# Paired row halves, kept x pieces, a held convolution and a joined start in a two-layer image kernel

## The chip, the cores and the metric

The kernel runs on one core of a Trainium2 chip. The metric is the device time of one execution in microseconds; the median of three executions stands for a kernel. A profile is one further execution, with its own time.

## The reference

Two layers, each `x + conv(groupnorm(x))` on `x` of 4 images x 192 channels x 128 x 128, all in fp32. Cut to what matters:

```python
# layer 0
x1 = _c1x1(x, conv1_w)                       # 192 -> 48 channels
x_0, x_05, x_1 = x1[:, :16], x1[:, 16:32], x1[:, 32:48]
Fre = _frft2d(x_05, 0.5)                     # fractional Fourier transform
mag, pha = abs(Fre), angle(Fre)
mag_out = _c1x1(_c3x3(mag * mask1) * mask1 + _c1x1(mag * mask2) * mask2)
ifrft = abs(_frft2d(complex(mag_out * cos(pha_out), mag_out * sin(pha_out)), -0.5))
fre = rfft2(x_1)                             # ordinary Fourier transform
x_1o = irfft2(...)                           # 1x1 convolutions of its magnitude and phase
x = x + _c1x1(concat([x_0o, ifrft, x_1o]), conv2_w)   # 48 -> 192 channels

# layer 1: a selective scan over the 16384 pixels of each image
seq = layernorm(groupnorm(x)); xs, z = split(seq @ in_proj)       # 384 + 384
u = silu(causal_conv4(xs)); dt, Bm, Cm = split(u @ x_proj)
dt = softplus(dt @ dt_proj + b)
h = h * exp(dt * A) + (dt * u) * Bm;  y = sum(h * Cm)             # 16 states
x = x + ((y + u * D) * silu(z)) @ out_proj
```

## The kernel before

**Layer 0** (`layer0`) works image by image, in generators that a loop at its end advances in turns. A scheduler then orders the recorded instructions on each engine; every engine, and every queue of an engine that issues transfers, works in the order that comes out. Nearly all loads are issued by SP, the stores of `d1` by ACT and the stores of `xmid` by POOL.

- `analysis(b)` has two passes over the image's 16 pieces of 8 rows (`PIECE` = 1024 pixels, two tiles of 96 channels side by side: 768 KB each). The first takes the group statistics (`bn`, line 192), the second loads every piece again and makes the 48 channels with line 278, whose matmuls use one column half of the array for each half piece. The result goes to `d1` in DRAM.
- `branches(b)` is the Fourier part. It has 26 steps (`yield`s): 8 in the forward transforms (lines 214 and 224, `spectrum`; the polar form of each half is lines 76 to 96, with the magnitude's sum on POOL, line 78), 4 in the convolutions (line 348 is the 3x3 one), 2 in the second branch's 1x1 convolutions, 8 in the inverse fractional transform (lines 407 to 421) and 4 in the inverse ordinary one (lines 437 to 448). It ends with the write of `dimg` to DRAM (line 453).
- `synthesis(b)` loads the x pieces a third time. For each piece it loads `cat`, which has 49 rows: 16 of `d1`, 32 of `dimg` and a row of ones (lines 464 to 466). Four matmuls with 49 rows (line 471) make 192 channels of 1024 pixels, DVE adds them to x (line 475), takes statistics for layer 1 (line 192), and POOL stores the piece to `xmid` (line 477).

All x pieces come from one pool of six tiles, `l0x`. While `branches(b)` runs, the loop advances `analysis(b+1)` once in every step and once more in odd steps, and `synthesis(b-1)` in even steps; what is left of both is flushed after it. For the last image there is no analysis ahead, so only the synthesis of image 2 runs beside its branches. `synthesis` of the last image runs alone.

**Layer 1** (`layer1`) has its order written out by hand. The 128 chunks of 512 pixels pass through `front` (a generator of 34 steps: normalisation, projections, convolution, `dt`), then 24 positions of scans. In the main loop `front(n+2)` starts at position 14 (`FRONT`) of chunk n, does ten steps there and the remaining 24 in the next chunk. To start, `front(0)` runs through, then the inputs of the first scans are prepared, and then ten steps of `front(1)` are done before the loop begins. `NGR` is 24.

Of the kernel before, what the change touches and what calls it, by code (L numbers as in the profile page):

```python
# [10 lines left out]
F32 = mybir.dt.float32  # L11
# [8 lines left out]
C = 192  # L20
CH = 96
GROUP = 6
NC = 16
# [9 lines left out]
PIECE = ROWS * S  # L33
NPIECE = S // ROWS
# [87 lines left out]
def layer0(tc, x, xmid, st2, w):  # L122

    nc = tc.nc
    B = x.shape[0]
    with ExitStack() as ctx:
# [10 lines left out]
        qp = pool("l0q", 1)  # L137
# [22 lines left out]
        nc.sync.dma_start(out=w2x[0:NC, :], in_=folded[0:NC, :])  # L160
        nc.sync.dma_start(out=w2x[3 * NC :, :], in_=folded[NC:, :])
        half_pi = cp.tile([128, 1], F32, name="half_pi")
        nc.vector.memset(half_pi, math.pi / 2)

# [4 lines left out]
        dmag = []  # L169
        zrow = cp.tile([1, S], F32, name="zrow")  # L170
        nc.vector.memset(zrow, 0.0)
        orow = cp.tile([1, PIECE], F32, name="orow")
        nc.vector.memset(orow, 1.0)
# [73 lines left out]
        def analysis(b, got):  # L247


            st = sp.tile([CH, 2, NPIECE * (PIECE // 512), 6], F32, name="st")  # L250
            for p in range(NPIECE):
                bn(st, p, load(b, p))
                yield
            gst = sp.tile([CH, 2, 2], F32, name="gst")
            bn_done(st, gst)

            w1r = sp.tile([CH, 2, 128], F32, name="w1r")
            for t in range(2):  # L260
                nc.vector.tensor_scalar(w1r[:, t, :], w1T[:, t, :], gst[:, t, 1:2], None, ALU.mult)
            ps = psA.tile([128, 512], F32, name="ps")
            for t in range(2):
                nc.tensor.matmul(
                    ps[:, 0:1], w1r[:, t, :], gst[:, t, 0:1], start=t == 0, stop=t == 1
                )
            b1 = sp.tile([128, 1], F32, name="b1")
            nc.vector.tensor_scalar(b1, ps[:, 0:1], -1.0, None, ALU.mult)
            d1 = got["d1"] = dram.tile([3 * NC, S * S], F32, name="d1")
            for p in range(NPIECE):  # L270
                xt = load(b, p)
                if p % 2 == 0:
                    x1 = sp.tile([128, 2, 512], F32, name="x1")
                ps = psA.tile([128, 512], F32, name="ps")
                for t in range(2):
                    for q in range(2):
                        half = slice(64 * q, 64 * (q + 1))
                        nc.tensor.matmul(
                            ps[half], w1r[:, t, half], xt[:, t, q * 512 : (q + 1) * 512],
                            start=t == 0, stop=t == 1,  # L280
                        )
# [171 lines left out]
            nc.sync.dma_start(out=dimg.rearrange("c h w -> h c w"), in_=img)  # L453
            got.update(dimg=dimg)

        def synthesis(b, got):

            d1, dimg = got["d1"], got["dimg"].rearrange("c h w -> c (h w)")
            st = sp.tile([CH, 2, NPIECE * (PIECE // 512), 6], F32, name="st2")
            for p in range(NPIECE):  # L460
                xt = load(b, p)
                cat = qp.tile([3 * NC + 1, PIECE], F32, name="cat", bufs=2)
                at = slice(p * PIECE, (p + 1) * PIECE)
                nc.sync.dma_start(out=cat[0:NC, :], in_=d1[0:NC, at])
                nc.sync.dma_start(out=cat[NC : 3 * NC, :], in_=dimg[:, at])
                nc.sync.dma_start(out=cat[3 * NC :, :], in_=orow)
                for q in range(PIECE // 512):
                    at = slice(q * 512, (q + 1) * 512)
                    pr = psB.tile([128, 2, 512], F32, name="pr")
                    for t in range(2):  # L470
                        nc.tensor.matmul(  # L471
                            pr[0:CH, t, :], w2x[:, t * CH : (t + 1) * CH], cat[:, at],
                            start=True, stop=True,
                        )
                    nc.vector.tensor_add(xt[:, :, at], xt[:, :, at], pr[0:CH])  # L475
                bn(st, p, xt)
                nc.gpsimd.dma_start(  # L477
                    out=split(xmid[b][:, p * PIECE : (p + 1) * PIECE]), in_=xt
                )
                yield  # L480
            bn_done(st, st2[:, b])
# [3 lines left out]
        got = [{} for _ in range(B)]  # L485
        for _ in analysis(0, got[0]):
            pass
        behind = iter(())
        for b in range(B):
            ahead = analysis(b + 1, got[b + 1]) if b + 1 < B else iter(())  # L490
            for i, _ in enumerate(branches(b, got[b])):
# [5 lines left out]
            behind = synthesis(b, got[b])  # L497
        for _ in behind:
            pass

# [3 lines left out]
def layer1(tc, xmid, out, st2, w, n_tok=S * S):  # L504

    nc = tc.nc
    B = len(xmid)
    NCHUNK = n_tok // T
    G = 2
    LAG, FRONT, BCL = 3, 14, 5  # L510
# [4 lines left out]
    MID, LATE = "mid", "late"  # L515
# [3 lines left out]
    with ExitStack() as ctx:  # L519
        def pool(name, bufs, **kw):  # L520
            return ctx.enter_context(tc.tile_pool(name=name, bufs=bufs, **kw))

        cp = pool("l1c", 1)
        dram = pool("l1d", 3, space=DRAM)
        xp = pool("l1x", 3)
# [66 lines left out]
        NG = NS // G  # L592
        NGR = NJ * NG
        got = [{} for _ in range(total)]
# [355 lines left out]
        fronts = []  # L950

        def start_front(n):
            if n < total:
                fronts.append(front(n))

        def step(works, parts):

            for f in list(works):
                got_on = next(f, f)
                if got_on is f:  # L960
                    works.remove(f)
                elif got_on is not None:
                    parts[got_on].append(f)

        def go_on(parts, part):

            for f in parts[part]:
                got_on = next(f, None)
                if got_on is not None:
                    parts[got_on].append(f)  # L970

        with tc.manual_schedule():
# [12 lines left out]
            decay_there(2)  # L985


            start_front(1)
            for _ in range(NGR - FRONT):
                parts = {MID: [], LATE: []}  # L990
                step(fronts, parts)
                go_on(parts, MID)
                go_on(parts, LATE)
            tails = []
            for pos, (n, k) in enumerate(order):
                j, sg = divmod(k, NG)
# [4 lines left out]
                parts = {MID: [], LATE: []}  # L1001
# [188 lines left out]
```

## Time and profile before

| | us |
|---|---|
| median of three executions | 11470.67 (11470.17 to 11471.05) |
| the profiled execution | 11449.58 |
| its span | 11447.4 |
| analysis of image 0 alone ends (load of `img` issued) | 126.4 |
| writes of `dimg`, images 0, 1, 2, 3 | 395.9, 699.2, 1029.8, 1302.6 |
| first constant of layer 1 | 1436.5 |
| first scan of layer 1 | 1515.3 |

Busy shares of the whole span are PE 92%, DVE 92%, POOL 86%, ACT 81%: those are layer 1's. In layer 0 the shares change from stretch to stretch, and must be read there. In lines of the timeline the columns are start, length, engine, line, operation, what is written and read, the shape and the count; in brackets is the idle time just before and what ended it. An engine name ending in q is that engine's issue queue. An fp32 matmul shows as two passes.

### The profile page before, as it was taken

To read this page: it belongs to the slowest core of one execution; us is meant where nothing else is said; L and a number is where in the kernel's file an instruction comes from. 1 tells how busy PE (TensorE), PEld (TensorE's weight loads), DVE (VectorE), ACT (ScalarE), POOL (GpSimd) and SP (SyncE) were. 2 spreads that over 40 slices of the span, in tenths; PEclk is the share of its full clock that TensorE was granted. 3 is DMA by queue.
4 is the path that set the end of the run, shared out by engine and by line. 5 is a ranking of instruction groups with operands and counts; after the bars stand their busy time and mean duration, and the time that the engine had idled before them with its cause. 6 is when DMAs were issued, how large, how long until landed. Compare 5 with 4: busy or idle time off the path is not lost.

```text
span 11447.4 us, 163662 instructions
## 1 busy us (share of the span) xinstructions
PE 10543.1 (92%) x54154; PEld 7050.4 (62%) x54154; DVE 10489.8 (92%) x11072; ACT 9324.7 (81%) x17508; POOL 9806.5 (86%) x4470
## 2 busy tenths in 40 slices
PE   4777889999999999999999999999999999999998
PEld 2444456666666666666666666666666666666666
DVE  5665679999999999999999999999999999999999
ACT  2322179988988998998998998898899999889887
POOL 0000069999999999999999999999999999999999
PEclk8888789999999999999999999999999999999998
DMA  8787734334334434434433433443443443344343
GB/s 209 206 223 203 196 106 128 112 119 128 118 113 128 127 106 130 128 107 124 128 112 119 128 120 111 128 127 105 129 128 109 123 128 114 117 128 121 111 128 99
DMA packets 1339431, 1494.73 MB, mean 131 GB/s; under 512 B 903473, under 2 KB 954358, under 8 KB 1338070
## 3 DMA queue, kind: packets, MB, share of 16 engines
q1 hardware_dynamic: 1318102, 1421.34, 42.7%
q0 software_dynamic: 13312, 50.34, 1.3%
q10 hardware_dynamic: 7168, 12.59, 0.3%
q8 instruction: 429, 7.03, 0.2%
q14 instruction: 420, 3.44, 0.1%
HBM read 1325.19 MB, written 155.32 MB: 129 GB/s over the span
## 4 chain that ended last, share of the span: by engine, by line
ACT 29%; DVE 29%; PE 26%; issue 10%; POOL 3%; DMA 2%; DVEq 0%; ACTq 0%; POOLq 0%; SPq 0%
DVE h L872 21%; ACT da L802 9%; ACT dbT L846 6%; DVE op L822 6%; PE py L898 5%; PE ps L666 4%; PE ps L936 4%; PE ps L685 4%; ACT L802 3%; PE op L858 2%; POOL db L830 2%; ACT op L802 2%; PE pr L471 2%; ACT L693 1%; PE ps L655 1%
## 5 line engine op out<-in xcount | busy, mean ns | idle before, releaser
L885 POOL TENSOR_TENSOR hc<-h,bc 128x1024 f32<-128x1024 f32 x3072 | 7196.8, 2373 | 230.7 <-PE ps L922 145.6
L872 DVE TENSOR_TENSOR_SCAN h<-da,carry,op 128x512 f32<-128x512 f32 x4216 | 5202.2, 1262 | 18.7 <-ACT da L802 7.1
L898 PEld LDWEIGHTS py<-ident,hc 128*128 128x128 f32 x24576 | 3001.5, 148 | 849.3 <-issue 685.1
L898 PE MATMUL py<-ident,hc 128*128 128x128 f32 x24576 | 3404.1, 285 | 29.9 <-ACT yt L907 17.5
L802 ACT ACTIVATE da<-dt,c_A_log 128x512 f32<-128x512 f32 x4352 | 2994.6, 724 | 184.3 <-DVE h L872 163.6
L872 DVE TENSOR_TENSOR_SCAN h<-op,carry,db 128x512 f32<-128x512 f32 x1736 | 2202.3, 1269 | 119.2 <-POOL db L830 115.2
L830 POOL TENSOR_TENSOR db<-dtu,bc 128x1024 f32<-128x1024 f32 x896 | 2136.3, 2384 | 5.6 <-DMA bc<-dbc 5.6
L822 DVE TENSOR_TENSOR op<-dp,bc 128x512 f32<-128x512 f32 x2816 | 1889.9, 671 | 32.2 <-ACT dp L785 32.2
L802 ACT ACTIVATE op<-dt,c_A_log 128x512 f32<-128x512 f32 x1792 | 1223.2, 683 | 679.7 <-DVE h L872 674.4
L846 ACT ACTIVATE dbT<-ps,bT 128x128 f32<-128x128 f32 x6144 | 1660.3, 381 | 0.0
L666 PE MATMUL ps<-s,c_wiT 96*128 96x512 f32 x3072 | 1520.9, 619 | 2.6 <-DVE s L660 2.6
L685 PE MATMUL ps<-xs,dcw 128*128 128x512 f32 x3072 | 1424.3, 592 | 1.5 <-ACT u L693 1.3
L858 PE MATMUL op<-ident,dbT 128*128 128x128 f32 x6144 | 1076.2, 295 | 109.9 <-DVE h L872 75.5
L858 PEld LDWEIGHTS op<-ident,dbT 128*128 128x128 f32 x6144 | 779.8, 151 | 405.5 <-ACT dbT L846 208.7
L666 PEld LDWEIGHTS ps<-s,c_wiT 96*128 96x128 f32 x3072 | 558.1, 199 | 467.2 <-issue 462.9
L802 ACT ACT_TABLE_LOAD x636 | 816.0, 1283 | 11.2
L685 PEld LDWEIGHTS ps<-xs,dcw 128*128 128x128 f32 x3072 | 532.9, 190 | 434.1 <-issue 432.1
L936 PE MATMUL ps<-yg,c_woT 128*96 128x512 f32 x1536 | 710.5, 598 | 71.1 <-DVE xm L942 70.9
L477 POOL DMA_DIRECT2D xmid<-xt x64 | 42.8, 668 | 788.1 <-DVE xt L475 781.3
L745 PE MATMUL ps<-xd,c_dtT 12*128 12x512 f32 x768 | 514.1, 761 | 164.5 <-DVE s L622 99.7
L936 PEld LDWEIGHTS ps<-yg,c_woT 128*96 128x96 f32 x1536 | 239.8, 163 | 437.8 <-issue 320.7
L754 POOL TENSOR_TENSOR dtu<-dt,u 128x512 f32<-128x512 f32 x384 | 479.4, 1282 | 29.6 <-ACT dt L750 29.6
(172 smaller groups left out, 10372.6 us busy)
## 6 DMA issues: line engine op xcount, KB each, us to landing
bc<-dbc SPq DMA_DIRECT2D x1024, 1024.0 KB, 5.9
xt<-in_x SPq DMA_DIRECT2D x192, 768.0 KB, 9.0
xmid<-xt POOLq DMA_DIRECT2D x64, 768.0 KB, 7.0
xm<-xmid SPq DMA_DIRECT2D x128, 384.0 KB, 3.5
carry<-h SPq DMA_DIRECT2D x3072, 1.0 KB, 1.9
out<-xm SPq DMA_DIRECT2D x128, 384.0 KB, 3.3
d<-x ACTq DMA_DIRECT2D x64, 192.0 KB, 7.1
df<-u SPq DMA_DIRECT2D x16, 512.0 KB, 5.2
```

The source lines that it names most:

```text
L666: nc.tensor.matmul(pp, wiT[:, t, m * 128 : (m + 1) * 128], s[:, t, :], start=t == 0, stop=t == 1)
L685: nc.tensor.matmul(pc, dcw[:, j, k, :], xs[:, j, k : k + T], start=k == 0, stop=k == 3)
L745: nc.tensor.matmul(d[j], dtT[rows, :], xd[rows, :], start=True, stop=True)
L802: nc.scalar.activation(da, got[n]["dt"][j], AF.Exp, scale=A[:, j, st : st + 1])
L822: nc.vector.tensor_tensor(dbs[s], g["dp"], g["bc", k % NG][:, 0, q, :], ALU.mult)
L830: nc.gpsimd.tensor_tensor(db, _bc(g["dtu"][j], 1, G), g["bc", sg][:, 0], ALU.mult)
L846: nc.scalar.activation(t[:, blk, :], g["tu", j][:, blk, :], AF.Identity, scale=g["bT"][:, blk, st : st + 1],)
L858: nc.tensor.transpose(db[:, blk * 128 : (blk + 1) * 128], t[:, blk, :], ident)
L872: nc.vector.tensor_tensor_scan(h[:, q, :], das.pop(s), dbs.pop(s) if db is None else db[:, q, :], 0.0 if ch == 0 else g["before"][:, j, st ...
L885: nc.gpsimd.tensor_tensor(hc, h, g["bc", sg][:, 1], ALU.mult)
L898: nc.tensor.matmul(py[:, blk, :], hc[:, q, blk * 128 : (blk + 1) * 128], ident, start=first, stop=sg == NG - 1 and q == G - 1 and blk == T ...
L936: nc.tensor.matmul(po[0:CH], woT[:, j, t * CH : (t + 1) * CH], g["yg", j], start=j == 0, stop=j == NJ - 1,)
```

## The change

Seven things are changed, none of them in what is computed.

1. **Row halves.** The two half pieces of 512 pixels of `cat` lie one above the other: rows 0 to 48 and rows 64 to 112 of one tile of 128 x 512. The weights `w2x` are there twice, in the same rows. For each 96 output channels, the matmuls of the two halves stand next to each other, and DVE then adds 1024 pixels of these channels at a time.
2. **Two fixed `cat` tiles**, filled with ones at the start, take the place of the pool's; the row of ones is not loaded any more. A piece has four `cat` loads of half the width (before: two, and the row).
3. **Kept x pieces.** The last four pieces of the first pass of `analysis` stay in their tiles and come first in the second pass. It loads 12 pieces where it loaded 16.
4. The x pool has seven tiles.
5. **Held synthesis.** In the last image, `synthesis` of image 2 is not advanced in the first ten steps of `branches`, and then in every step.
6. **Early loads.** At step 18 of the last image's branches the first four x pieces of the last synthesis are loaded.
7. **Layer 1's start.** The ten first steps of `front(1)` are done between those of `front(0)`, from its 19th step on, and the first loads of `bc` are issued there.

```diff
-        xp = pool("l0x", 6)
+        xp = pool("l0x", 7)
...
-        w2x = cp.tile([3 * NC + 1, C], F32, name="w2x")
-        nc.sync.dma_start(out=w2x[NC : 3 * NC, :], in_=w["w2T"][NC:, :])
+        w2x = cp.tile([128, C], F32, name="w2x")
+        for q in range(2):
+            nc.sync.dma_start(out=w2x[64 * q + NC : 64 * q + 3 * NC, :], in_=w["w2T"][NC:, :])
...
+        cats = [cp.tile([128, 512], F32, name=f"cat{i}") for i in range(2)]
+        for cat in cats:
+            nc.vector.memset(cat, 1.0)
...
+            kept = {}
             for p in range(NPIECE):
-                bn(st, p, load(b, p))
+                xt = load(b, p)
+                if p >= NPIECE - KEEP:
+                    kept[p] = xt
+                bn(st, p, xt)
...
-            for p in range(NPIECE):
-                xt = load(b, p)
+            for p in (*range(NPIECE - KEEP, NPIECE), *range(NPIECE - KEEP)):
+                xt = kept.pop(p, None) or load(b, p)
...
-        def synthesis(b, got):
+        def synthesis(b, got, early):
...
-                xt = load(b, p)
-                cat = qp.tile([3 * NC + 1, PIECE], F32, name="cat", bufs=2)
-                at = slice(p * PIECE, (p + 1) * PIECE)
-                nc.sync.dma_start(out=cat[0:NC, :], in_=d1[0:NC, at])
-                nc.sync.dma_start(out=cat[NC : 3 * NC, :], in_=dimg[:, at])
-                nc.sync.dma_start(out=cat[3 * NC :, :], in_=orow)
-                for q in range(PIECE // 512):
-                    at = slice(q * 512, (q + 1) * 512)
+                xt = early[p] if p < len(early) else load(b, p)
+                cat = cats[p % 2]
+                for q in range(2):
+                    at = slice(p * PIECE + q * 512, p * PIECE + (q + 1) * 512)
+                    nc.sync.dma_start(out=cat[64 * q : 64 * q + NC, :], in_=d1[0:NC, at])
+                    nc.sync.dma_start(out=cat[64 * q + NC : 64 * q + 3 * NC, :], in_=dimg[:, at])
+                for t in range(2):
                     pr = psB.tile([128, 2, 512], F32, name="pr")
-                    for t in range(2):
+                    for q in range(2):
+                        rows = slice(64 * q, 64 * q + 3 * NC + 1)
                         nc.tensor.matmul(
-                            pr[0:CH, t, :], w2x[:, t * CH : (t + 1) * CH], cat[:, at],
+                            pr[0:CH, q, :], w2x[rows, t * CH : (t + 1) * CH], cat[rows, :],
                             start=True, stop=True,
                         )
-                    nc.vector.tensor_add(xt[:, :, at], xt[:, :, at], pr[0:CH])
+                    nc.vector.tensor_add(
+                        xt[:, t, :], xt[:, t, :], pr[0:CH].rearrange("p q f -> p (q f)")
+                    )
...
             for i, _ in enumerate(branches(b, got[b])):
                 next(ahead, None)
-                next(ahead if i % 2 else behind, None)
+                if b < B - 1 or i >= HOLD:
+                    next(ahead if i % 2 and b < B - 1 else behind, None)
+                if b == B - 1 and i == LOADS:
+                    early = [load(b, p) for p in range(KEEP)]
...
-            for _ in front(0):
-                pass
-            for sg in range(NG):
-                load_bc(0, sg)
+            first = [front(0)]
+            for i in range(2 * NGR - FRONT):
+                if i == NGR - 6:
+                    start_front(1)
+                once(first)
+                if NGR - 6 <= i < 2 * NGR - FRONT - 6:
+                    once(fronts)
+                if i == NGR + 1:
+                    for sg in range(NG):
+                        load_bc(0, sg)
...
-            start_front(1)
-            for _ in range(NGR - FRONT):
-                parts = {MID: [], LATE: []}
-                step(fronts, parts)
-                go_on(parts, MID)
-                go_on(parts, LATE)
```

`KEEP` is 4, `HOLD` 10 and `LOADS` 18. `once` is the body of the loop that was removed: one step of each generator in a list, with its middle and late parts.

More of the change, by code (lines that the diff above doesn't have):

```diff
@@ L125, in layer0 @@
     B = x.shape[0]
+    KEEP = 4
+    HOLD = 10
+    LOADS = 18
     with ExitStack() as ctx:
@@ L159, in layer0 @@
         nc.vector.tensor_copy(folded, ps[0 : NC + 1, 0:C])
-        nc.sync.dma_start(out=w2x[0:NC, :], in_=folded[0:NC, :])
-        nc.sync.dma_start(out=w2x[3 * NC :, :], in_=folded[NC:, :])
+        for q in range(2):
+            nc.sync.dma_start(out=w2x[64 * q : 64 * q + NC, :], in_=folded[0:NC, :])
+            nc.sync.dma_start(
+                out=w2x[64 * q + 3 * NC : 64 * q + 3 * NC + 1, :], in_=folded[NC:, :]
+            )
         half_pi = cp.tile([128, 1], F32, name="half_pi")
@@ L171, in layer0 @@
         nc.vector.memset(zrow, 0.0)
-        orow = cp.tile([1, PIECE], F32, name="orow")
-        nc.vector.memset(orow, 1.0)
+        cats = [cp.tile([128, 512], F32, name=f"cat{i}") for i in range(2)]
+        for cat in cats:
+            nc.vector.memset(cat, 1.0)
         for i in range(min(2, B)):
@@ L460, in synthesis @@
             for p in range(NPIECE):
-                xt = load(b, p)
-                cat = qp.tile([3 * NC + 1, PIECE], F32, name="cat", bufs=2)
-                at = slice(p * PIECE, (p + 1) * PIECE)
-                nc.sync.dma_start(out=cat[0:NC, :], in_=d1[0:NC, at])
-                nc.sync.dma_start(out=cat[NC : 3 * NC, :], in_=dimg[:, at])
-                nc.sync.dma_start(out=cat[3 * NC :, :], in_=orow)
-                for q in range(PIECE // 512):
-                    at = slice(q * 512, (q + 1) * 512)
+                xt = early[p] if p < len(early) else load(b, p)
[5 more added lines that the diff above has]
+                for t in range(2):
                     pr = psB.tile([128, 2, 512], F32, name="pr")
-                    for t in range(2):
+                    for q in range(2):
+                        rows = slice(64 * q, 64 * q + 3 * NC + 1)
                         nc.tensor.matmul(
-                            pr[0:CH, t, :], w2x[:, t * CH : (t + 1) * CH], cat[:, at],
+                            pr[0:CH, q, :], w2x[rows, t * CH : (t + 1) * CH], cat[rows, :],
                             start=True, stop=True,
                         )
-                    nc.vector.tensor_add(xt[:, :, at], xt[:, :, at], pr[0:CH])
+                    nc.vector.tensor_add(
+                        xt[:, t, :], xt[:, t, :], pr[0:CH].rearrange("p q f -> p (q f)")
+                    )
                 bn(st, p, xt)
@@ L490, in layer0 @@
             ahead = analysis(b + 1, got[b + 1]) if b + 1 < B else iter(())
+            early = []
             for i, _ in enumerate(branches(b, got[b])):
                 next(ahead, None)
-                next(ahead if i % 2 else behind, None)
+                if b < B - 1 or i >= HOLD:
+                    next(ahead if i % 2 and b < B - 1 else behind, None)
+                if b == B - 1 and i == LOADS:
+                    early = [load(b, p) for p in range(KEEP)]
             for rest in (behind, ahead):
@@ L496, in layer0 @@
                     pass
-            behind = synthesis(b, got[b])
+            behind = synthesis(b, got[b], early)
         for _ in behind:
@@ L970, in go_on, with once @@
                     parts[got_on].append(f)
+        def once(works):
+            parts = {MID: [], LATE: []}
+            step(works, parts)
+            go_on(parts, MID)
+            go_on(parts, LATE)
         with tc.manual_schedule():
@@ L974, in layer1 @@
                 load_x(i)
-            for _ in front(0):
-                pass
-            for sg in range(NG):
-                load_bc(0, sg)
+            first = [front(0)]
[8 more added lines that the diff above has]
+                        load_bc(0, sg)
+            assert not first, first
             dtu_copy(0, 0)
```

## The prediction

> **What bounds the kernel now.** I read the page's forty slices first, then busy time by stretch, then the chain of waits in each stretch, then the timeline where that chain turns odd.
>
> ```profile
> PE   4777889999999999999999999999999999999998
> PEclk8888789999999999999999999999999999999998
> DMA  8787734334334434434433433443443443344343
> ```
>
> A slice is 286 us. From the sixth on PE is at 9 to the end: that is layer 1's loop, from the first scan at 1515.3 us. The changed program's instruction order from that scan on is the old one on all five engines, so its 9,932 us stay; everything edited lies in the first 1,515 us.
>
> ```profile
> 126.00:396.00 270.00, 181.31 (x727) 114.75 (x728) 154.01 (x193) 91.43 (x126) 13.97 (x11) 0.83 0.80 202
> 396.00:699.00 303.00, 234.49 (x777) 124.69 (x776) 174.71 (x204) 87.30 (x119) 23.28 (x24) 0.83 0.78 202
> 699.00:1030.00 331.00, 252.77 (x831) 133.59 (x830) 208.36 (x263) 89.84 (x123) 23.98 (x27) 0.82 0.85 223
> 1030.00:1302.00 272.00, 224.94 (x703) 127.92 (x703) 176.04 (x199) 76.65 (x104) 24.39 (x28) 0.81 0.62 169
> 1302.00:1436.00 134.00, 114.69 (x143) 37.84 (x141) 89.96 (x119) 0.20 (x1) 11.41 (x18) 0.51 0.74 215
> ```
>
> Columns: length, busy PE, weight load, DVE, ACT, POOL, granted clock, DMA share, GB/s. The cuts are the writes of `dimg` that end each image's branches, so these are images 0 to 3 and the last synthesis. Before 126 us image 0 is analysed alone at a DMA share near 1.0. No engine fills images 0 to 3: they run on chains through PE, ACT, DVE and POOL. In the last stretch PE does nothing but line 471, at half clock:
>
> ```profile
> 396.00:699.00 303.00, 63.15 (x110) 18.28 (x111) 0.83 0.78 202
> 699.00:1030.00 331.00, 74.05 (x131) 21.19 (x130) 0.82 0.85 223
> 1030.00:1302.00 272.00, 81.35 (x139) 23.16 (x139) 0.81 0.62 169
> 1302.00:1436.00 134.00, 113.22 (x136) 36.63 (x134) 0.51 0.74 215
> ```
>
> These are line 471's matmuls alone. What one costs, against matmuls that share the array:
>
> ```profile
> 340.38 1.94 PE L278 MATMUL ps<-xt,w1r 96*64 96x512 f32 x8
> ...
> 1068.24 3.67 PE L471 MATMUL pr<-cat,w2x 49*96 49x512 f32 x8
> ...
> 1399.70 30.07 PE L471 MATMUL pr<-cat,w2x 49*96 49x512 f32 x35
> ...
> 1486.86 1.13 PE L745 MATMUL ps<-xd,c_dtT 12*128 12x512 f32 x6 [0.68 <-ACT xd L734]
> ```
>
> Eight passes of line 278, two column halves at a time, take 1.94 us; eight of line 471 take 3.67, or 6.8 in the last stretch (859 ns a pass). Line 745 takes 1.13 us for six passes in three row groups: row groups run side by side too. While image 3 is in its branches, POOL reads:
>
> ```profile
> 1100.11 1.03 POOL L477 DMA_DIRECT2D xmid<-xt  x1 [17.65 <-DVE xt L475]
> 1109.19 2.35 POOL L78 TENSOR_TENSOR u<-u 128x1024 f32<-128x1024 f32 x1 [8.05 <-ACT u L77]
> ...
> 1138.02 0.63 POOL L477 DMA_DIRECT2D xmid<-xt  x1 [22.30 <-DVE xt L475]
> 1143.94 2.63 POOL L78 TENSOR_TENSOR u<-u 128x1040 f32<-128x1040 f32 x1 [5.29 <-ACT u L77]
> ```
>
> The magnitude sum (line 78), which the branches need, stands behind stores of image 2's synthesis that wait for DVE. And layer 1's start:
>
> ```profile
> 1500.26 1.50 ACT L612 ACTIVATE s<-xm,nmr,st 96x512 f32<-96x512 f32 x2
> ...
> 1514.16 1.22 DVE L660 TENSOR_TENSOR s<-s,ps 96x1024 f32<-96x1024 f32 x1 [2.83 <-PE ps L655]
> 1515.30 2.32 DVE L872 TENSOR_TENSOR_SCAN h<-da,op 128x512 f32<-128x512 f32 x2
> ```
>
> Chunk 1's ten front steps fill 1500.3 to 1515.3, with DVE otherwise idle; the first scan comes after them.
>
> **What the Trainium skill says.** "TensorE: Matmul & The Clock Gate", Part 3 (packing small matmuls): matmuls in different row groups run concurrently; line 745's 1.13 us agrees. "TensorEngine Tiling (Array Packing)", Gotcha 1: row tiles must not write one PSUM bank together; the change gives the two halves different 512-column slices, and no run here yet shows the pair. The clock page's Part 1 has a busy array go to full clock; the trace disagrees, with PE busy 20 of 20 us at 0.50 between 1340 and 1420 us, so I count on no faster clock. "DMA: Bandwidth & Descriptors", Issuing engines are not separate DMA queues: all queues share 16 engines. That fits: shares above 0.9 go with 250 to 275 GB/s whichever queue is at work.
>
> **The change, part by part** (times against the profiled execution).
>
> *Start, 0 to 126 us.* Four of image 0's 32 loads go: 4 x 0.786 MB at 260 GB/s = 12 us, all on the path since DMA is full. Three more small SP issues near the first loads cost 0.45 us each, +1.4. Four of the seven x tiles stay occupied while the statistics are finished, so three loads run ahead instead of six: 9 us of transfers against a chain of about 6, no loss. Sum -10.6.
>
> *Images 0, 1, 2.* Line 471 has 7.6% of the chain in image 1's stretch (23.0 us) and 7.1% in image 2's (23.5). A pair of passes at the price of one halves that: -11.5 and -11.7. The four dropped loads (12 us of DMA time each) are mostly beside PE work: image 0's chain from 300 to 363 us has no load in it. What they can shorten is the wait for `u<-df`, 14.8 to 15.5 us on the chain with x loads queued, where such a transfer's median over the stage is 11.1: -3 in each. The extra SP issue per synthesis piece (four `cat` loads for three) is 0.4 us, hidden behind SP's waits of 261 us on line 471. The DVE adds keep their size (1024 elements, 1.21 us). Sums -3, -14.5, -14.7.
>
> *Image 3, held synthesis.* With no store before it, line 78 runs when ready. From the first transform to the first 3x3 convolution took 87 us (1059.98 to 1146.8); five synthesis pieces in it cost DVE 5 x 4.9 = 24.5 (two adds of 1.21, four statistics of 0.64). -25, with the POOL waits inside it. Then up to 1237 us both orders carry eight pieces; PE pays 8 x 1.8 us less, about 40% of it on the chain: -6. From 1237 to 1302 the old order carries three pieces, the new one eight. PE there goes from 3 x 3.67 = 11.0 to 8 x 1.85 = 14.8 us. DMA was 31 us busy; five pieces more (8.85 MB) and the four early loads (3.1 MB) at 290 GB/s add 41, so 72 into 65: with some latency, +10. Sum -21.
>
> *Last synthesis, 1302 to 1436 us.* The 17.7 us until `dimg` is written and read back stay. PE's 6.8 us a piece fall to 3.4 even at half clock, so PE stops setting the pace. Next is DVE at 4.9, or DMA: 1.77 MB a piece, 0.98 for the first four. In 1400 to 1420 us DMA was 0.89 busy at 268 GB/s, so about 300 when full: 12 x 5.9 + 4 x 3.3 = 84 us; DVE needs 78. I take 88 and 2 us for a store backlog in front of layer 1's constants, against 114.4: -24. Bounds: 79 (DVE alone) and 105 (each piece waiting for its `cat` at the median 3.5 us behind a load of 9), so -33 to -7.
>
> *Layer 1's start.* The 15 us go. Into front(0), where PE is busy without a break from 1471 to 1486, come PE's statistics (3.6), transposed rows (2.4), mean (1.9) and projection (1.9), with table loads of 1.28 beside them: 9 us later. -6, bounds -12 to +3.
>
> Sum: 10.6 + 3 + 14.5 + 14.7 + 21 + 24 + 6 = 93.8, which I take as 92. The profiled execution took 11449.58 us (span 11447.4 and 2.2 around it), so 11357.6. The median of the runs shown, 11470.67, lies 21.1 above; subtracting from it gives 11378.7.
>
> **Rivals.** *DMA takes the place of PE.* For it: shares of 0.95 to 1.05 in 300 to 400 and 600 to 620 us, and 84 us of transfers in the tail; against it: 0.62 over image 3. Then images 1 and 2 gain only the dropped traffic (6 each), image 3 gains 8, the tail 10: 10.6 + 3 + 12 + 8 + 10 + 6 = 50, so 11421.
>
> *The row halves don't run side by side.* Line 745 speaks against it, though its groups have 12 rows and not 49. The tail keeps 109 us of PE, image 1 to 3 lose 11.5 + 11.7 + 6, and eight late pieces cost 15 us more PE: 92 - 24 - 29 - 15 = 24, so 11447.
>
> *Slower: early loads starve the synthesis.* From branch step 18 four of seven x tiles belong to image 3, so image 2's last eight pieces share three. A tile's turn is load 9.0, DVE 5, store 7.0: 21 us, or 7 a piece over three tiles, 56 us for eight and inside my 75. PE is in order, so if loads and stores slow each other, the transforms behind line 471 wait. It decides only when eight pieces need 75 + 92 us, 21 a piece, three times what the page's landings give. At 24 a piece: 192 - 75 = 117, so 11496.
>
> That the program doesn't do what it says is ruled out for the order: the first three line-78 sums of image 3 now stand ahead of its synthesis' stores.
>
> **How the numbers follow.** Forecast 11379, chance 0.68, own range 11325 to 11415; DMA rival 0.20; no overlap 0.05; starved 0.04; nothing measurable otherwise 0.03. 0.2% is 23 us, about what a measurement of this kernel tells from no change. No overlap falls on that line, so half of it is "same": faster 0.90, same 0.06, slower 0.04. Range: 11325 (tail and start at their good bounds, 16 more, and up to 38 from images 1 and 2 where SP waits shorten) to 11435 (beyond the DMA rival).
>
> **What would show it.** Right: line 471's successor takes about half the time for its 512 passes' work; the gap from the last `dimg` write to layer 1's first constant near 110 us; first image transformed near 115 us; first scan about 92 us earlier. Wrong: pairs that do not overlap in time, DMA at 1.0 through the tail with more than 6 us a piece, PE idle behind `pr` between the inverse transforms, or a changed time for the loop after the first scan.

## The result, and the profile after

The changed kernel took 11381.78 us (median of 4 executions, 11376.91 to 11396.82) where the kernel before took 11470.42 (4 executions, 11464.68 to 11471.05): ratio 0.9926, 95% interval 0.9909 to 0.9943. The forecast was 11379, with a range of 11325 to 11435.

The stages below end at the same events as before: the load of `img`, the four writes of `dimg` (line 467 now), the first constant of layer 1 and its first scan (line 892). The stage from the last `dimg` write to the first constant is called the tail, and the one after the first scan the loop. Both kernels were profiled a second time in the experiments, and both profiles are given, since single stages repeat only within some us.

| stage | before, us | after, us | mean change | predicted |
|---|---|---|---|---|
| analysis of image 0 alone | 126.4, 127.9 | 125.5, 124.8 | -2.0 | -10.6 |
| image 0 | 269.5, 269.2 | 265.5, 264.3 | -4.5 | -3 |
| image 1 | 303.3, 301.1 | 299.2, 301.4 | -1.9 | -14.5 |
| image 2 | 330.5, 331.5 | 322.5, 321.5 | -9.0 | -14.7 |
| image 3 | 272.8, 269.6 | 258.3, 255.0 | -14.6 | -21 |
| last `dimg` write to first constant | 133.9, 133.8 | 105.3, 105.9 | -28.3 | -24 |
| first constant to first scan | 78.8, 78.4 | 69.1, 68.5 | -9.8 | -6 |
| first scan to end | 9932.1, 9939.8 | 9938.2, 9937.6 | +2.0 | 0 |

Up to the first scan that is 70 us, not the 92 of the sum. The medians moved further than the profiles, by 88.6 us here and by 82.1 in the second comparison below, because the profiled executions of the kernel before (11449.6 and 11453.4) lie at the low end of its runs (11451 to 11472 over all sessions). No single place for that surplus was found; the first profile's loop was 8 us shorter than the second's, and 5.7 us of that grew evenly from the first scan to the last. So the total was met closely, but partly by luck: the sum of the stages was 22 us too large.

The changed kernel by stretch, columns as before (length, busy PE, weight load, DVE, ACT, POOL, clock, DMA share, GB/s):

```profile
391.00:690.00 299.00, 226.43 (x792) 121.56 (x790) 181.58 (x217) 88.24 (x120) 23.86 (x25) 0.83 0.76 202
690.00:1013.00 323.00, 239.30 (x827) 129.86 (x828) 201.18 (x253) 89.87 (x123) 23.66 (x27) 0.80 0.82 215
1013.00:1067.00 54.00, 37.80 (x174) 30.00 (x172) 34.45 (x37) 24.94 (x36) 6.84 (x4) 0.87 0.51 139
1067.00:1271.00 204.00, 159.96 (x528) 84.29 (x528) 144.60 (x162) 51.63 (x68) 18.16 (x24) 0.82 0.69 184
1271.00:1376.00 105.00, 72.08 (x138) 24.07 (x136) 84.10 (x115) 0.20 (x1) 10.70 (x17) 0.52 0.85 259
```

These are images 1 and 2, the two parts of image 3 (divided at the load of `magQ`, the magnitude that the convolutions read), and the last synthesis. PE has 8 and 13 us less to do in images 1 and 2, which are only 2 and 9 us shorter. The matmuls of line 485 (line 471 before) alone took, in images 1 and 2:

```profile
391.00:690.00 299.00, 50.14 (x120) 12.46 (x120) 0.83 0.76 202
690.00:1013.00 323.00, 52.74 (x127) 12.73 (x128) 0.80 0.82 215
```

That is 50.1 and 52.7 us in place of 63.2 and 74.1, not half of them. The last stretch lost 28 us with its clock still at half. Its timeline on the changed kernel, PE and then DVE:

```profile
1312.96 3.80 PE L485 MATMUL pr<-cat,w2x 49*96 49x512 f32 x8 [0.51 <-DVE xt L489]
1317.59 3.80 PE L485 MATMUL pr<-cat,w2x 49*96 49x512 f32 x8 [0.83 <-DVE xt L489]
```

```profile
1311.70 2.33 DVE L489 TENSOR_TENSOR xt<-xt,pr 96x1024 f32<-96x1024 f32 x2
1313.95 2.46 DVE L202 BATCH_NORM_STATS2 st<-xt 96x6 f32<-96x512 f32 x4
1316.34 2.33 DVE L489 TENSOR_TENSOR xt<-xt,pr 96x1024 f32<-96x1024 f32 x2
1318.59 2.46 DVE L202 BATCH_NORM_STATS2 st<-xt 96x6 f32<-96x512 f32 x4
```

Eight passes take 3.80 us where they took 6.8: the pairs do run side by side, at a clock of 0.50. Now PE waits for DVE, which has no gap, and a piece takes 4.63 us (from 1312.96 to 1317.59). Later pieces wait for `cat` loads instead: between 1330 and 1350 us the DMA share was 0.99. That is the prediction's picture of the tail, 88 us forecast for it and 85 measured from the first matmul (1290) to the end of the last piece (1375).

### The profile page after: what moved, and what is told of

It is laid out like the page before. It is cut to its first block, busy times and chain, and to the rows that moved or that the text cites. A ratio compares the mean times of both kernels' runs of the same rounds, so it can differ in the third digit from the quotient of the medians.

```text
span 11383.6 us, 163735 instructions
## 1 busy us (share of the span) xinstructions
PE 10442.3 (92%) x54154; PEld 7012.0 (62%) x54154; DVE 10486.9 (92%) x11073; ACT 9317.9 (82%) x17507; POOL 9813.9 (86%) x4470
## 4 chain that ended last, share of the span: by engine, by line
DVE 31%; ACT 29%; PE 27%; issue 8%; DMA 3%; POOL 2%; DVEq 0%; SPq 0%; POOLq 0%; ACTq 0%
DVE h L892 21%; ACT da L822 9%; ACT dbT L866 6%; PE py L918 6%; DVE op L842 5%; PE ps L686 4%; PE ps L705 4%; PE ps L956 4%; ACT L822 3%; PE op L878 2%; ACT op L822 2%; ACT L713 1%; POOL db L850 1%; PE ps L675 1%; ACT dt L770 1%
## 5 line engine op out<-in xcount | busy, mean ns | idle before, releaser
L892 DVE TENSOR_TENSOR_SCAN h<-op,carry,db 128x512 f32<-128x512 f32 x1736 | 2201.1, 1268 | 128.5 <-POOL db L850 123.9
L842 DVE TENSOR_TENSOR op<-dp,bc 128x512 f32<-128x512 f32 x2816 | 1886.6, 670 | 11.5 <-ACT dp L805 11.5
```

Of the source, the lines that this page charges most:

```text
L842: nc.vector.tensor_tensor(dbs[s], g["dp"], g["bc", k % NG][:, 0, q, :], ALU.mult)
L892: nc.vector.tensor_tensor_scan(h[:, q, :], das.pop(s), dbs.pop(s) if db is None else db[:, q, :], 0.0 if ch == 0 else g["before"][:, j, st ...
```

## The experiments

The times are medians of 4 or 5 executions (13 for the kernel before, run again), each compared with the kernel before in the same session (its medians were 11460.68, 11460.13 and 11468.3). Executions of one kernel lie 5 to 21 us apart, and the last `dimg` write of three profiles with the same layer-0 code (two of the changed kernel, one with layer 1's old start) came at 1260.8 to 1271.0 us. Smaller differences show nothing by themselves.

**The changed kernel again** (no edit).

> The changed kernel once more, to learn how far the stage times of one program repeat. Theory (the two profiles differ by less than the medians only because a long loop varies from one execution to the next): the first constant of layer 1 comes within 3 us of 1376.3 and the first scan within 3 us of 1445.4, while the time from the first scan to the end may differ from 9938 by up to 10 us. Rival (the change makes the loop itself 6 us longer): the loop takes 9938 within 2 us again. Ratio to the kernel before: 0.992 to 0.993 in both.

11378.6 us (11376.5 to 11381.0), ratio 0.9927 (0.9915 to 0.9940). First constant at 1372.9, first scan at 1441.4, loop 9937.6. The layer-0 stages repeat within 4 us here; in the third profile with this layer-0 code image 3 took 250.7 us, 4 to 8 less. The loop did come out the same, but the kernel before, run again below, had 9939.8 as well: the change does not lengthen it.

**Without the side-by-side.**

```
-        w2x = cp.tile([128, C], F32, name="w2x")
+        w2x = cp.tile([128, 2, C], F32, name="w2x")
+        nc.vector.memset(w2x, 0.0)
...
-                        rows = slice(64 * q, 64 * q + 3 * NC + 1)
+                        rows = slice(0, 64 + 3 * NC + 1)
...
-                            pr[0:CH, q, :], w2x[rows, t * CH : (t + 1) * CH], cat[rows, :],
+                            pr[0:CH, q, :], w2x[rows, q, t * CH : (t + 1) * CH], cat[rows, :],
```

> The changed kernel, with both row halves multiplied by weights of 113 rows in which the other half's rows are zero: loads, order, adds and the number of passes stay, only the side-by-side of two halves goes. Theory A (the pairs are worth most in the last synthesis, where DVE's 4.63 us a piece then give way to PE's 6.8, and little in images 1 to 3, where other chains end last): last dimg write to first constant 105.3 -> 125 to 130 us, images 1, 2 and 3 together +3 to +10 us, whole kernel +25 to +35 us, 11407 to 11417. Theory B (my prediction's own terms: line 471's share of the chain in images 1 and 2 is time): images 1 and 2 +10 us each, image 3 +15, tail +22: whole kernel +57, about 11439.

11390.4 us (11377.5 to 11394.6), 12 above the changed kernel: less than both theories. Images 1 and 2 got *shorter* (291.1 and 316.6 us against 301.4 and 321.5), image 3 longer (268.3), and the tail took only 115.4 us. Stretches of its last synthesis show why (columns as above):

```profile
1288.00:1308.00 20.00, 15.62 (x32) 5.21 (x30) 17.04 (x22) 0.00 (x0) 2.19 (x4) 0.92 0.61 174
1308.00:1328.00 20.00, 16.32 (x31) 5.69 (x32) 15.07 (x20) 0.00 (x0) 2.21 (x4) 0.83 0.78 238
```

The clock, 0.50 in the kernel before with PE 100% busy, is 0.92 and 0.83 here with PE 80% busy. The only change to these matmuls is 113 rows in place of 49. At full clock the unpaired passes cost 3.67 us a piece (from 1301.69 us, for one), no more than pairs at half clock (3.80). So this edit took the side-by-side away and raised the clock at once, and it can't say what the pairs are worth at an unchanged clock.

**Without kept pieces** (`KEEP` zero in `analysis`; the four early loads stay).

> The changed kernel without kept pieces: the second pass loads all 16 again, from seven tiles; the four early loads of the last synthesis stay. Theory A (in image 0 the four saved loads are given back as DMA idle time while three free tiles are full and the kept ones wait for the statistics): the load of img comes at 125 to 127 us, as with the kept pieces (125.5); images 1 and 2 lengthen by up to 3 us each; whole kernel 0 to +8 us, 11382 to 11390. Theory B (the kept pieces do save their 12 us of DMA, and the seventh tile or the added loads at the start took it back elsewhere): the load of img comes at 136 us or later, images 1 and 2 +6 to +12 each, whole kernel +22 to +34.

11383.9 us (11380.2 to 11384.8), 5 above the changed kernel. The load of `img` came at 128.5 us, between the theories. Image 0 took 270.9 us in place of 264.9 (mean of two), image 1 291.1 in place of 300.3, image 2 320.4, and the last `dimg` write came at 1261.5, not later than with the kept pieces (1267.0 and 1271.0). What they save in the start and in image 0, some 9 us, image 1 gives back. The start's own loss is visible in the changed kernel's stretches:

```profile
60.00:70.00 10.00, 0.00 (x0) 0.00 (x0) 8.39 (x14) 0.00 (x0) 0.00 (x0) 1.00 1.03 254
70.00:80.00 10.00, 7.32 (x18) 3.08 (x20) 2.38 (x10) 0.20 (x1) 0.00 (x0) 1.00 0.34 86
80.00:90.00 10.00, 10.00 (x48) 3.32 (x46) 0.00 (x0) 2.75 (x4) 0.00 (x0) 1.00 0.88 243
```

Between 70 and 80 us, DMA is busy 0.34 of the time (1.03 in the kernel before): by the program, three free tiles are full then and four wait for the statistics.

**Without the held synthesis.**

```
-                if b < B - 1 or i >= HOLD:
-                    next(ahead if i % 2 and b < B - 1 else behind, None)
+                next(ahead if i % 2 else behind, None)
```

> The changed kernel with the synthesis of image 2 advanced in every second step of the last image's branches from the first on, as before. Theory A (POOL's line 78 again stands behind the stores of xmid, and the late crowding goes): from the third dimg write to the load of magQ 54.7 -> about 80 us, from there to the last dimg write 203.7 -> about 190 us, whole kernel +10 to +15 us. Theory B (the first half's gain is given back in the second entirely): third to fourth dimg write within 3 us of 258.4, whole kernel 0 within 4.

11373.9 us (11369.1 to 11375.7), 5 *below* the changed kernel, so neither theory. The hold shortens the first part of image 3 (54.7 us from `dimg` to `magQ`, 66.7 without) and lengthens the second by more (203.6 and 200.3, and 180.8 without); the tail is 3 us shorter with it. Over five profiles with the hold and pairs, image 3 took 249.6 to 258.3 us; over five without it, 244.6 to 247.5. With 64 rows (below) the two versions end layer 0 within 1 us of each other, so the hold brings nothing, and may cost a few us.

**Sixty-four rows in each half** (the weights' spare rows are zero).

```
+        nc.vector.memset(w2x, 0.0)
...
-                        rows = slice(64 * q, 64 * q + 3 * NC + 1)
+                        rows = slice(64 * q, 64 * q + 64)
```

> The changed kernel with 64 rows in each half's matmul instead of 49 (rows 49 to 63 have weights of zero): pairs stay side by side, with the same number of passes. Measured so far: the granted clock of the last synthesis was 0.50 with 49 rows and 0.83 to 0.92 with 113 (no_pair). Theory A (the clock follows how much of the array is at work, and pairs of 64 rows count as 128): clock of the last synthesis above 0.8, last dimg write to first constant 105 -> 100 to 104 us, since DVE (4.63 us a piece) and DMA stay; images 1 and 2 each 5 to 10 us shorter at a clock of 0.87; whole kernel -10 to -25 us against the changed one, 11354 to 11369. Theory B (what counts is the rows of a single instruction, and 64 are still too few): the clock stays 0.50 and all times stay within 3 us of the changed kernel's.

11373.0 us (11366.8 to 11376.2), ratio 0.9922 (0.9909 to 0.9936). Clock of the last synthesis 0.71, between the theories; tail 104.7 us, since DVE and DMA stay. Images 1 and 2 took 298.5 and 321.8: theory A's 5 to 10 us there did not come, and neither did its clock: 0.84 and 0.81 over them, where the changed kernel had 0.83 and 0.80.

**The kernel before with 128 rows.** Nothing else of the change, except that the ones stand in two fixed tiles and are not loaded.

```
-        w2x = cp.tile([3 * NC + 1, C], F32, name="w2x")
+        w2x = cp.tile([128, C], F32, name="w2x")
+        nc.vector.memset(w2x, 0.0)
...
+        cats = [cp.tile([128, PIECE], F32, name=f"cat{i}") for i in range(2)]
+        for cat in cats:
+            nc.vector.memset(cat, 1.0)
...
-                cat = qp.tile([3 * NC + 1, PIECE], F32, name="cat", bufs=2)
+                cat = cats[p % 2]
...
-                nc.sync.dma_start(out=cat[3 * NC :, :], in_=orow)
```

> The kernel before, with the 49 rows of the synthesis' matmuls filled up to 128 (weights of zero), two fixed tiles with the ones in them in place of the pool's, and no load of the row of ones. Nothing else of the change. Theory A (the granted clock follows the rows at work): in the last synthesis the clock rises from 0.50 to 0.8 or more, PE falls from 6.8 to about 4 us a piece, DVE's 4.9 is next: last dimg write to first constant 133.9 -> 108 to 116 us; images 1 to 3 each 3 to 8 us shorter; whole kernel 11418 to 11440. Theory B (the clock falls where PE works without a break, whatever the rows; no_pair's 0.9 came of its pauses): the clock stays at 0.50 in the last synthesis, the tail stays within 5 us of 133.9, whole kernel within 10 us of before.

11410.6 us (11409.1 to 11417.4), ratio 0.9958 (0.9946 to 0.9971): theory A for the clock, with a gain beyond its range, though image 2 did not get shorter (332.1 us). Its last synthesis:

```profile
1330.00:1350.00 20.00, 16.59 (x33) 5.49 (x33) 16.63 (x21) 0.00 (x0) 1.89 (x4) 0.90 0.77 235
1350.00:1370.00 20.00, 13.31 (x30) 4.32 (x28) 19.86 (x27) 0.00 (x0) 2.90 (x5) 1.00 1.02 347
1370.00:1390.00 20.00, 16.06 (x32) 5.39 (x32) 16.87 (x22) 0.00 (x0) 2.13 (x4) 0.91 0.90 302
```

At clocks of 0.90 to 1.00 the tail takes 105.9 us, the same as the changed kernel's 105.3 and 105.9, without pairs and without early loads. So the tail's 28 us are the end of a PE limit, which pairs at half clock and single passes at a higher clock both lift. Two things stay open. The kernel with 113 single rows had nearly this clock, and its tail took 115.4 us. And the first matmul of the last synthesis comes 13.35 us after the `dimg` write here and 18.4 in the changed kernel, which then needs 87 us to the first constant where this one needs 92.5; the early loads may be worth those 5 us or so, and no run takes them out alone.

Theory B's unbroken work does not by itself lower the clock: in the stretches of the changed kernel's start above, PE is busy all of 80 to 90 us at a clock of 1.00, with 96-row matmuls. The images are 8 to 11 us shorter in all (last `dimg` write 1291.1 against 1302.6 and 1299.2).

**Layer 1's old start, and the kernel before again.**

> The changed kernel with the start of layer 1 as before: front(0) alone, then the first scans' inputs, then ten steps of front(1). Theory A (my step, mis-sized): first constant to first scan 68.5 -> 78 to 79 us, the time after the first scan stays at 9938, whole kernel +9 to +11 us, 11388 to 11390. Theory B (the 5.5 us by which the loop is longer in every changed kernel come from that start): first scan 10 us later, but the loop goes back to 9932, whole kernel +4 to +5 us.

11387.3 us (11385.5 to 11391.2), 8.7 above the changed kernel; first constant to first scan 78.1 us, loop 9938.2: theory A.

> The kernel before once more, for how far its stages repeat. Theory A (the stages of layer 0 repeat within 3 us, the loop within 3): dimg writes near 396, 699, 1030 and 1303 us, first scan near 1515, loop 9929 to 9935. Theory B (its profiled execution was a short one by chance, which is why the profiles differ by less than the medians): first scan or loop together 10 to 20 us longer than in the first profile.

11462.8 us, ratio 1.0001 (0.9993 to 1.0009). Layer 0 repeated within 4 us, as in theory A; the loop took 9939.8, not 9929 to 9935, and first scan and loop together came out 4 us longer, not 10 to 20: neither theory.

**Neither kept pieces nor hold, with seven and with six tiles.**

> The changed kernel without kept pieces and without the held synthesis, both at once; the pairs, the fixed tiles with the ones, seven x tiles, the early loads and layer 1's start stay. Alone, each of the two left the end of layer 0 where it was: the last dimg write came at 1261 (keep_none) and 1255 us (no_hold), against 1261 to 1271 in three profiles of this layer-0 code. Theory A (neither gains anything): last dimg write 1250 to 1271 us, whole kernel 11370 to 11386. Theory B (each covers for the other): last dimg write 1280 to 1295, whole kernel 11395 to 11410.

11385.3 us (11376.0 to 11392.1), last `dimg` write at 1268.9: theory A.

> The run before (neither), with six x tiles and three early loads, so that three tiles are left to image 2's last pieces as there. Theory A (the seventh tile is what shortened images 0 to 3): last dimg write 1285 to 1300 us, near the 1299 to 1303 of the kernel before; whole kernel 20 to 35 us above the seven-tile run. Theory B (the pairs and the dropped load of ones did it, tiles are enough): last dimg write within 6 us of the seven-tile run, tail +3 for the load that is not early, whole kernel +2 to +8.

11378.2 us (11375.3 to 11383.1), last `dimg` write at 1256.1, 13 us *earlier* than with seven tiles, against theory A and beyond theory B's 6 us: nothing speaks for the seventh. This kernel holds only the rewritten synthesis (pairs, fixed tiles, no load of ones), three early loads and layer 1's start, and it is as fast as the changed one.

What in the rewritten synthesis shortens images 2 and 3? From the write of `dimg` to the first transform of the next image took 29.0 and 30.2 us in the kernel before (images 2 and 3), 30.4 and 30.0 in the one with 128 rows, 30.2 and 28.9 without the side-by-side, and 13.3 and 13.3 in the changed one; the other paired kernels, but for the last below, had 10.9 to 13.3. SP and PE around the third `dimg` write, first without the side-by-side:

```profile
999.75 0.38 SPq L467 DMA_DIRECT2D dimg<-img  x1
1000.18 9.06 SPq L480 DMA_DIRECT2D cat<-dimg  x1
...
1015.31 6.79 PE L485 MATMUL pr<-cat,w2x 113*96 113x512 f32 x8 [13.57 <-DMA cat<-dimg]
...
1028.65 2.91 PE L224 MATMUL ps<-c_fr,img 128*128 128x256 f32 x6
```

and then the changed kernel's second profile:

```profile
1006.62 0.42 SPq L480 DMA_DIRECT2D cat<-dimg  x1
...
1011.97 0.38 SPq L467 DMA_DIRECT2D dimg<-img  x1
1012.44 8.29 SPq L479 DMA_DIRECT2D cat<-d  x3
...
1015.36 1.10 PE L485 MATMUL pr<-cat,w2x 49*96 49x512 f32 x4 [0.67 <-DVE xt L489]
...
1025.22 2.06 PE L224 MATMUL ps<-c_fr,img 128*128 128x256 f32 x4
```

Without pairs, a load of `cat` for the last piece of the synthesis under way stands *behind* the 2 MB write in SP's order. Its issue takes 9.06 us, though its tile had been free for 7, and it lands at 1015.2 us, 0.2 after the write. PE reaches that piece before the transform and waits 13.57 us for it. In the changed kernel the loads behind the write belong to the next synthesis, and PE needs none of them before the transform; of the 8.29 us that three of them take to issue, 4.1 are SP's wait for PE to free the first one's tile. Counting SP's instructions for images 1 and 2: in the kernel before and in the one with 128 rows the loads of one whole piece stand behind each of the two writes, without the side-by-side those of a whole piece and then one load of four; in the changed kernel and in the other paired ones, none. The scheduler, given the new synthesis, had placed these loads ahead. Image 2's and image 3's first parts, from `dimg` to `magQ`, fell from 84 to 68 us and, without the hold, from 85 to 67. No run moves these loads alone, so this cause is read from the traces. Against it as the whole of image 2's gain stands the kernel without the side-by-side: its image 2 starts as late as before and, at a higher clock, is still 14 us shorter than before (316.6 against 331.0).

**Combined versions.** The 64 rows without the hold:

> The changed kernel with 64 rows in each half and without the held synthesis. Theory A (the higher clock and the earlier start of image 2's pieces add up): last dimg write 1243 to 1252 us, last write to first constant 105 to 109, whole kernel 11360 to 11368. Theory B (both shorten the same waits): last dimg write 1253 to 1260 us, whole kernel 11369 to 11376.

11372.9 us (11363.5 to 11377.5), last `dimg` write at 1254.1: theory B.

Then the blocking write made smaller:

```
             nc.scalar.activation(img[:, 0:NC, :], img[:, 0:NC, :], AF.Sqrt)
+            dimg = dram.tile([2 * NC, S, S], F32, name="dimg")
+            rows = dimg.rearrange("c h w -> h c w")
+            nc.sync.dma_start(out=rows[:, 0:NC, :], in_=img[:, 0:NC, :])
...
+                if q % 2:
+                    at = slice(NC + 4 * q - 4, NC + 4 * q + 4)
+                    nc.sync.dma_start(out=rows[:, at, :], in_=img[:, at, :])
                 yield
-            dimg = dram.tile([2 * NC, S, S], F32, name="dimg")
-            nc.sync.dma_start(out=dimg.rearrange("c h w -> h c w"), in_=img)
```

> As pair64_nohold, with dimg written in three parts as its channels are done: 16 channels before the ordinary inverse transform, then 8 and 8. Theory A (the 9.6 us until 2 MB of dimg have landed stand on the path between the last branch and the last synthesis, and only the last 0.5 MB need to): first matmul of the last synthesis 5 to 7 us sooner after the last dimg write, so last write to first constant 98 to 103 us, images 0 to 2 the same, whole kernel -5 to -8 us against pair64_nohold. Theory B (SP works in order, and the two added writes hold back the loads of cat and x behind them): images 1 and 2 longer by 3 to 6 us each, whole kernel 0 to +8.

11353.4 us (11344.5 to 11365.9), ratio 0.9902 (0.9888 to 0.9915), against 0.9927 for the changed kernel: the fastest of all, 19.5 us below the run before it in the same session: theory A for the tail, and more than its 5 to 8 us. Images 0 to 2 did not stay as they were, but their differences (+3, -12 and +3 us, and +4 at the start) nearly cancel. Its last synthesis begins:

```profile
1252.38 0.38 SPq L471 DMA_DIRECT2D dimg<-img  x1
...
1262.02 1.99 PE L490 MATMUL pr<-cat,w2x 64*96 64x512 f32 x2 [8.54 <-issue]
```

The first matmul comes 9.6 us after the last write, where the run before it, without the split, took 21.4 (1254.1 to 1275.5) and the changed kernel 18.4 (1270.96 to 1289.4). The tail is 100.5 us in place of 110.6, and the first scan 12 us earlier; the remaining 7 us of the medians' difference are not placed.

## Why the prediction was right, and which steps were not

*Tail, -24:* right in mechanism, -28.3 measured. PE stopped setting the pace, DVE (4.63 us a piece) and then DMA took over, with the clock still half. What the prediction did not see is that the half clock itself came with the 49 rows: 128 rows give the same tail.

*Images 1 and 2, -14.5 and -14.7:* the step "A pair of passes at the price of one halves that: -11.5 and -11.7" failed. The pairs did not halve line 471's work there: its own PE time fell to 0.79 and 0.71 of what it was, since only 84 of 120 and 88 of 127 passes run beside another; between the halves of the others the scheduler had put other matmuls. And line 485 still has 6.2% and 7.0% of the chain (18.5 and 22.6 us), 4.8% and 7.1% in the second profile. Such a share was a weak guide: for line 471 over image 1 it is 7.1% to 7.6% in the first profile of the kernel before, by where the stretch ends, and 8.8% in the second; and 42% of that chain is "issue", time in which an engine waited for nothing that the profile shows. What the pairs are worth in these images stays open. Without the side-by-side, images 1 and 2 were together 15 us *shorter* than with it, but at clocks of 0.88 and 0.87 between `magQ` and `dimg` against 0.82 and 0.80. Image 2 starts its transforms 16 us earlier, where SP's order changed, and the rest of it is 7 us longer. Image 1 was 7 to 11 us shorter than before in the three paired kernels without kept pieces, so its 2 us are what the kept pieces left.

*Start, -10.6:* failed at "Four of the seven x tiles stay occupied ... no loss". The chain that I put at 6 us left DMA two thirds idle for 10 us. The kept pieces save 3 to 8 us against the same start without them (128.5 and 133.3 us, in two kernels), and only 2 against the kernel before.

*Image 3, -21:* a size, and half a cause. The first part became 31 and 29 us shorter (predicted -25), but only 12 of them by the hold, and 17 to 19 are there without it; of these, 15 to 17 lie before the first transform, where SP's order changed. The second part became 17 and 15 us longer where "-6" and "+10" made 4. Without the hold it is 5 us shorter than before, so the late crowding came to some 20, twice what I put on it, and the hold brings nothing.

*Layer 1's start, -6:* a size, -9.8, within its bounds; the old start alone gives 9.2 back. So the joined steps cost front(0) some 5 us, and not 9. *Image 0, -3:* -4.5. *Loop, 0:* right.

The rival "DMA takes the place of PE" gave images 1 and 2 12 us together, and 11 were measured; but DMA's share was 0.76 and 0.82 there, and its tail (-10) was wrong. Of the signs for "right", the gap (105 us for "near 110") and the cheaper passes came; the load of `img` at 125 us (for "near 115") and a first scan 70 us earlier (for "about 92") did not. Of the signs for "wrong", pairs that do not overlap appeared in images 1 to 3 for three passes in ten, and DMA near 1.0 in the tail for one stretch of 20 us.

One reading of the prediction does not hold: DMA shares above 0.9 do not go with 250 to 275 GB/s throughout. The kernel before moved 309 GB/s at 1.03 from 100 to 120 us and 192 at 1.02 from 840 to 860, and from 300 to 320 us its share was 0.81. The tail's rate, "about 300 when full", was near: 317 at a share of 0.99.

Not settled: what pairs alone bring in images 1 to 3, why kept pieces lengthen image 1 by 5 to 10 us, why the tail with 113 single rows is 10 us longer than with 128, and where the kernel before loses the 10 us that its timed executions have over its profiled ones.

## What to carry to other kernels

Read the granted clock of a stretch beside the rows of its matmuls: filling 49 rows up to 128 with zero weights, and not loading a row of ones, gave 50 of the change's 82 us by the medians (34 of 68 by the profiled executions). In an order made by a scheduler, look for small loads behind a large write on the same issue queue before believing a share of the chain of waits, and make such writes smaller. Undo each part of a change alone: three of seven here (kept pieces, seventh tile, hold) could be taken out together, with one of the four early loads, at no loss.

## What the runs showed of the hardware

In a stretch with almost no other matmuls, the granted clock went with the rows of the fp32 matmuls. This is the last synthesis, from its first matmul to its end:

| rows of a matmul | busy share of PE | clock |
|---|---|---|
| 49, single (before) | 0.95 | 0.50 |
| 49, in pairs (changed) | 0.83 | 0.50 |
| 64, in pairs (64 rows; and without hold) | 0.67; 0.69 | 0.71; 0.65 |
| 113, single | 0.71 | 0.88 |
| 128, single | 0.71 | 0.89 |

Each clock is a mean: in the kernel with 128 rows it is 1.00 from 1310 to 1327 us, 0.50 to 1333.8, and 1.00 again to 1371. The busiest PE has the lowest clock, in part because passes at half clock take longer. What sets the clock is not shown beyond this: pairs of 49 rows did not raise it, and pairs of 64 did for part of the time. The Trainium skill, "TensorE: Matmul & The Clock Gate", Part 1, says that the clock is gated by how busy the PE has been and is full after some 3.4 us of sustained work; over 116 us with PE 95% busy on 49 rows it stayed at half here, so the measurement decides. Pairs of row halves overlap in full when they stand together: at half clock eight passes took 3.80 us where single ones took 6.8.

After a write of `dimg` (2 MB from 128 partitions, landed 9.3 to 15.5 us after its issue where the trace tells), the next issue of SP took 5.4 to 9.1 us in the six places where the tile it wrote was free already; the median of the changed kernel's `cat` loads is 0.4. With 0.5 MB as the last write, the issue behind it took 0.3 to 1.0 us, and the first matmul of the last synthesis came 12 us sooner.
